# A gated two-part layer (state-space mixer, then a spiking feed-forward): the mixer's output computed feature-major in 512 columns, its second norm fetched through memory

## The chip, the cores and the metric

The kernel runs on one core of a Trainium2 chip. The core has five engines, each with its own queue of instructions, which it takes in order: TensorE (PE: matmuls, with its weight loads PEld), VectorE (DVE), ScalarE (ACT), GpSimd (POOL) and SyncE (SP), which here only issues DMAs. Operands lie in SBUF (128 partitions); matmuls write to PSUM, whose banks hold 128 x 512 fp32 values. The time is device microseconds (us) of one execution, lower is better. It is given as the median of several runs, and one further execution is profiled.

## The reference

For 16 sequences of 1024 tokens with 256 features, in fp32 (cut; the modulation `sa ... gb` is computed per sequence from a small input `c`, and `ga`, `gb` are clipped to at least 0.25 in size):

```python
h = _layernorm(x) * (1 + ca) + sa
Bu = (einsum('bti,ni->btn', h, W_B) + b_B) * dt          # 256 x 256
xs: x_t = A_bar * x_(t-1) + Bu_t                          # scan along the tokens
y = einsum('btn,on->bto', xs, W_C) + b_C + einsum('bti,oi->bto', h, W_D) + b_D
x = x + ga * y                                            # x1 below
h = _layernorm(x) * (1 + cb) + sb
y = square(relu(h @ W_fc.T)) @ W_proj.T                   # 256 -> 1024 -> 256
spikes: 5 steps of a leaky integrator driven by y, mean number of spikes per element
x = x + gb * spikes
```

## The kernel before

**Tiles.** The 16,384 tokens are cut into 32 tiles of 512 tokens (`TT`); two tiles make one sequence, and the scan carries its last column from the first to the second. Weights stay in SBUF, each as two fp32r halves (a rounded high part and the rest), and so do the moving operands: a product is three matmuls (`PASSES`: high x high, low weight x high, high weight x low) for each of the two 128-row blocks of the contraction (`products`, line 243).

**Layouts.** "Token-major" has tokens on the partitions, which the norm needs (its mean is along the free axis, `bn_stats`). "Feature-major" has features on the partitions, which matmuls, scan and the spike stage need. Two ways lead from one to the other. `transpose` (line 388) uses TensorE against an identity; it serves tiles 0 and 1 only. `hop` (line 342), through `turned` (line 346), has VectorE transpose 32 x 32 blocks, writes the result to device memory in four DMAs of 128 KB, and reads it back in one of 512 KB.

**The stages of a tile t**, by the names of the tiles in the profile:
- first norm of `xq` (a second copy of x in memory, laid out for `hop`): `moments`, `aggregate`, `root_in`, `root`, `root_inverse`, `newton`, `normalise` (xn_a, ScalarE), `hop` (w_a, hop_a, v_a), then `turned_hi` and `turned_lo` (lines 379, 382) give h_a, scaled, in two halves
- `state_input` (pb, 12 matmuls of 512 columns), `state_bias` (bu, ScalarE), `state_scan` (xs, VectorE), `state_hi` and `state_lo` (xsp)
- `mix_h` and `mix_xs` (lines 449, 455; py): here h_a and xsp stand as weights, in blocks of 128 tokens, and W_D and W_C move in 256 columns; y is token-major, in two PSUM tiles of 256 tokens (g = 0, 1). Each of the two makes 2 x 12 = 24 matmuls
- `residual` (line 398): GpSimd adds the bias row ga*(b_C + b_D + ...) to the loaded x, in place. `mix_out` (line 458): VectorE multiplies y by the row ga and adds that x: x1, token-major. The rows come broadcast over the partitions by `load_rows` (line 233) from a small table that the kernel writes at its start
- second norm of x1, by the same functions, and `hop` (w_b, hop_b, v_b), giving h_b
- `expand` (pf, 4 pairs of 2 x 6 matmuls; relu, square and the high half on ScalarE) with `hidden_lo` (hid, VectorE), and `contract` (pp, 4 pairs of 12 matmuls)
- `spike` (o, five VectorE operations for each half of the features), `gated` (ScalarE), and `output` (line 526; GpSimd adds x1, SyncE stores). `output` needs x1 feature-major, which `hop_residual` (line 359: w_x, hop_x, v_x) fetches by the same way as `hop`

**Order.** Nothing is left to a scheduler: all engines' handles are wrapped so that what is issued stays in program order (`InOrder`; so nearly all instructions in the profile have its line, 82). After set-up and a hand-written `first_period` (line 719), `period(t)` (line 839) is called for t = 1 to 30. It interleaves the stages of five tiles: spike, gate and output of t-1, expand and contract of t, second norm of t+2 with its hop in the next period, mix_xs and mix_out of t+2, state and mix_h of t+3, first norm of t+4. `last_tile` finishes. On TensorE a period reads: expand 0, expand 1, mix_xs, expand 2, contract 0, contract 1, expand 3, state_input, contract 2, mix_h, contract 3.

**Buffers.** PSUM: four banks `ps_f` (pf, pb), two `ps_y` (py), two `ps_p` (pp). `contract(t, 0)` therefore waits until both spikes of t-1 have read their pp. SyncE's queue is in order too: a DMA that waits for its data holds up those behind it.

Of the kernel before, what the change touches and what calls it, by code (L numbers as in the profile page):

```python
# [21 lines left out]
F32 = mybir.dt.float32  # L23
# [64 lines left out]
def adaln_kernel(ctx: ExitStack, tc: tile.TileContext, x, xq, w_bT, w_cT, w_dT, b_CD, w_fcT, w_projT,  # L88
                 cols, wmod, out):
# [19 lines left out]
    xts, xqs, bcs = {}, {}, {}  # L109

    def load(t):
        if t >= TILES:
            return
        xts[t] = io.tile([P, SUB, D], F32, tag="x", name=f"x_{t}", bufs=3)
        Q.dma_start(out=xts[t], in_=x[t])
# [9 lines left out]
    col = const.tile([P, KD * NB + 2 * KD + 1], F32, name="col")  # L125
    Q.dma_start(out=col, in_=cols)
    cs = col[:, 0:KD * NB].rearrange("p (k b) -> p k b", k=KD)
    la = col[:, KD * NB:KD * NB + KD]
    bb = col[:, KD * NB + KD:KD * NB + 2 * KD]
    ldt = col[:, KD * NB + 2 * KD:]  # L130
# [3 lines left out]
    load(0)  # L134
# [6 lines left out]
    spare = work.tile([NB, 8, D], F32, tag="hid", name="spare", bufs=HIDB)  # L141
    bcd, rows = spare[0:2, 0], spare[:, 2:5]
    Q.dma_start(out=fcm, in_=w_cT.rearrange("(k p) n -> p k n", p=P))
    Q.dma_start(out=bcd, in_=b_CD.rearrange("(n d) -> n d", n=2))
    load(1)
# [4 lines left out]
    load(2)  # L150
# [5 lines left out]
    first = spare[:, 5, 0:P]  # L156
    G.memset(first, 0.0)
    G.memset(first[0:1], 1.0)
    ones = spare[0:2, 7, 0:NB]
    G.memset(ones, 1.0)  # L160
# [11 lines left out]
    sb = const.tile([P, KD, NB], F32, name="sb")  # L172
    gb = const.tile([P, KD, NB], F32, name="gb")
# [5 lines left out]
    rows_a = dram.tile([NB, 2 * D], F32, name="rows_a")  # L179
# [40 lines left out]
    def gate(wm, name):  # L220
        ps = ps_f.tile([NB, D], F32, tag="ps_f", name=f"ps_{name}")
        for k in range(KD):
            PE.matmul(ps, lhsT=sil[:, k], rhs=wm[:, k, 2 * D:], start=k == 0, stop=k == KD - 1)
        return ps

# [6 lines left out]

    def load_rows(b):
        bc = io.tile([P, 2, D], F32, tag="bc", name=f"bc_{b}", bufs=2)
        Q.dma_start(
            out=bc.rearrange("p n d -> p (n d)"),
            in_=rows_a[b:b + 1, :].rearrange("o e -> (o e)").partition_broadcast(P),
        )
        bcs[b] = bc
# [18 lines left out]

    def moments(key, src, between=lambda: None, blocks=range(SUB)):
        if key not in norms:  # L260
            n = norms[key] = Norm()
            n.sts = [small.tile([P, 6], F32, tag=f"st{s}{key[0]}", name=f"st_{key}_{s}", bufs=2)
                     for s in range(SUB)]
        for s in blocks:
            V.bn_stats(norms[key].sts[s], src[:, s])
            between()
# [56 lines left out]
    def normalise(key, src):  # L323

        n = norms.pop(key)
        xn = work.tile([P, SUB, D], F32, tag="xn", name=f"xn_{key}", bufs=3)
        for s in range(SUB):
            S.activation(xn[:, s], src[:, s], AF.Identity, bias=n.m[:, s:s + 1], scale=n.r[:, s:s + 1])
        xns[key] = xn

    def normalise_by(key, src, engines):
# [3 lines left out]
        for s, E in enumerate(engines):  # L335
            if E is S:
                S.activation(xn[:, s], src[:, s], AF.Identity, bias=n.m[:, s:s + 1], scale=n.r[:, s:s + 1])
            else:
                E.tensor_scalar(xn[:, s], src[:, s], n.r[:, s:s + 1], n.m[:, s:s + 1], ALU.mult, ALU.add)
        xns[key] = xn  # L340

    def hop(key):

        vs[key] = turned(key, xns.pop(key), "turned", 3)

    def turned(key, src, tag, bufs):


        w = work.tile([P, D // 32, SUB, 32], F32, tag="xn", name=f"w_{key}", bufs=3)
        V.transpose(w.rearrange("p j s u -> p s j u"), src.rearrange("p s (j r) -> p s j r", r=32))  # L350
# [4 lines left out]
        v = work.tile([P, KD, TT], F32, tag=tag, name=f"v_{key}", bufs=bufs)  # L355
        Q.dma_start(out=v, in_=d.rearrange("(k p) t -> p k t", p=P))
        return v

    def hop_residual(t):
        xfs[t] = turned(f"x{t}", x1s.pop(t), "xf", 2)  # L360
# [27 lines left out]
    def transpose(key, pool=ps_f, tag="ps_f"):  # L388

        xn = xns.pop(key)  # L390
        for k in range(KD):
            ps = pts[key, k] = pool.tile([P, TT], F32, tag=tag, name=f"pt_{key}_{k}")
            for s in range(SUB):
                PE.transpose(ps[:, s * P:(s + 1) * P], xn[:, s, k * P:(k + 1) * P], ident)

    ys, vs, xns, hs, xbs, xss, xsps, x1s, xfs, relus, hids, accs, outs = ({} for _ in range(13))

    def residual(t, half, E=G):

        b = t // 2  # L400
        xt = xbs[t] = xts[t]
        xt = xt[:, 2 * half:2 * half + 2]
        E.tensor_tensor(xt, xt, bcs[b][:, 1:2].to_broadcast([P, 2, D]), ALU.add)
# [35 lines left out]
    def mix_part(t, g, w, a, first, last):  # L439


        for late in range(2):
            for j in range(2):
                cols = slice((2 * g + j) * P, (2 * g + j + 1) * P)
                products(ys[t, g][:, j], lambda i, k: w[:, i, k], lambda i, k: a[:, i, k, cols],
                         first and j == 0 and not late, last and late == 1, False,
                         PASSES[2:] if late else PASSES[:2], True)

    def mix_h(t, g):
        if g == 0:  # L450
            x1s[t] = work.tile([P, SUB, D], F32, tag="x1", name=f"x1_{t}", bufs=3)
        ys[t, g] = ps_y.tile([P, 2, D], F32, tag="ps_y", name=f"py_{t}_{g}")
        mix_part(t, g, wd, hs[f"a{t}"], True, False)

    def mix_xs(t, g):
        mix_part(t, g, wc, xsps[t], False, True)

    def mix_out(t, g):

        b = t // 2  # L460
        dst = x1s[t][:, 2 * g:2 * g + 2]
        V.tensor_tensor(dst, ys.pop((t, g)), bcs[b][:, 0:1].to_broadcast([P, 2, D]), ALU.mult)
        V.tensor_tensor(dst, dst, xbs[t][:, 2 * g:2 * g + 2], ALU.add)


    def expand_begin(t, pair):
# [9 lines left out]
        def rest(part):  # L476
            if part == 0:
                for j in range(2):
                    src, dst = ps[j], a[:, j]
                    if t == 0:  # L480
                        src = src.rearrange("p (s q u) -> p q s u", q=P // 32, s=SUB)
                        dst = dst.rearrange("p (q s u) -> p q s u", q=P // 32, s=SUB)
                    S.activation(dst, src, AF.Relu, bias=bias_f[:, 2 * pair + j, b:b + 1])
# [42 lines left out]
    def output(t, at, E=G):  # L526
# [4 lines left out]
        if E is G:  # L531
            G.tensor_tensor(o, o, xfs[t][:, m, cols], ALU.add)
        else:
            V.scalar_tensor_tensor(o, o, gb[:, m, b:b + 1], xfs[t][:, m, cols], ALU.mult, ALU.add)
        Q.dma_start(out=out[t, :, m, cols], in_=o)

    def last_tile(t):
# [4 lines left out]
        hop_residual(t)  # L542
# [72 lines left out]
    moments("a0", xts[0], between=lambda: decay(1))  # L615
# [15 lines left out]
    normalise_by("a0", xts[0], (V, S, V, S))  # L631
# [8 lines left out]
    ps_ga = gate(wm1, "ga")  # L640
    scaled_lo("a0", lambda k: pts["a0", k])
    V.tensor_tensor(wd[:, 1], fd, wd[:, 0].bitcast(F32), ALU.subtract)
    clipped(ps_ga, rows[:, 0], spare[:, 6], 1.0)
    S.activation(wc[:, 0], fcm, AF.Copy)
    state_input(0)

    ps_bd = ps_p.tile([NB, D], F32, tag="ps_p", name="ps_bd")
    PE.matmul(ps_bd, lhsT=ones, rhs=bcd, start=True, stop=False)
    for k in range(KD):
        PE.matmul(ps_bd, lhsT=sa[:, k], rhs=fd[:, k], start=False, stop=k == KD - 1)  # L650
    state_bias(0)
    state_scan(0, (0,))
    V.tensor_tensor(rows[:, 1], ps_bd, rows[:, 0], ALU.mult)
    Q.dma_start(out=rows_a, in_=rows[:, 0:2].rearrange("b n d -> b (n d)"))
    load_rows(1)
    mix_h(0, 0)

    ps_bc = ps_p.tile([P, 2, D], F32, tag="ps_p", name="ps_bc")
    PE.matmul(ps_bc.rearrange("p n d -> p (n d)"), lhsT=first, rhs=rows[:, 0:2].rearrange("b n d -> b (n d)"),
              start=True, stop=True)  # L660
    mix_h(0, 1)
# [5 lines left out]
    bcs[0] = io.tile([P, 2, D], F32, tag="bc", name="bc_0", bufs=2)  # L667
    S.activation(bcs[0], ps_bc, AF.Copy)
    state_lo(0, slice(1, 2))
    for half in range(2):  # L670
        residual(0, half, V)
    mix_xs(0, 0)
    mix_out(0, 0)
    moments("b0", x1s[0], blocks=(0, 1))
    mix_xs(0, 1)
    mix_out(0, 1)
    ps_cb = columns(wm2, 1, "cb")
    ps_sb = columns(wm2, 0, "sb")
    S.activation(sb, ps_sb, AF.Copy)
    moments("b0", x1s[0], blocks=(2, 3))  # L680
# [4 lines left out]
    moments("a1", xts[1], blocks=(0, 1))  # L685
    newton_v("b0")
    V.tensor_scalar(s2, ps_cb, 1.0, None, ALU.add)
    normalise_by("b0", x1s[0], (V, S, V, S))
# [3 lines left out]
    ps_bf = ps_p.tile([P, KF, NB], F32, tag="ps_p", name="ps_bf")  # L692
# [12 lines left out]
    moments("a1", xts[1], blocks=(2, 3))  # L705
# [11 lines left out]
    load(3)  # L717

    def first_period():
# [4 lines left out]
        normalise_by("a1", xts[1], (V, S, V, S))  # L724
# [3 lines left out]
        moments("a2", xqs[2])  # L728
        aggregate("a2")
        hop_residual(0)  # L730
# [7 lines left out]
        for half in range(2):  # L738
            residual(1, half)
# [9 lines left out]
        normalise("a2", xqs[2])  # L749
        hop("a2")  # L750
        load_q(4)
        for half in range(2):
            residual(2, half)
        for g in range(2):
            mix_h(1, g)
# [6 lines left out]
        moments("a3", xqs[3])  # L762
# [4 lines left out]
        halves(wp, fp, *proj(1))  # L767
        halves_lo(wp, fp, *proj(1), V)
        halves(wf, ff, *fc(3))
        halves_lo(wf, ff, *fc(3), V)  # L770
        r2(2)
        for g in range(2):
            mix_xs(1, g)
# [3 lines left out]
        for g in range(2):  # L777
            mix_out(1, g)
        contract(0, 1)
        normalise("a3", xqs[3])  # L780
        hop("a3")
        load_q(5)
        moments("b1", x1s[1])
        aggregate("b1")
        root_in_v("b1")
        root("b1")
        newton_v("b1")
# [177 lines left out]
```

## Time and profile before

| | |
|---|---|
| median of 3 runs | 1027.45 us (1024.75 to 1027.96) |
| profiled execution, its own time | 1027.32 us |
| its span, first to last instruction | 1025.5 us |
| mean granted TensorE clock | 0.991 |
| ScalarE busy | 771.9 us (75%) |
| GpSimd busy | 387.9 us (38%) |
| mean DMA traffic | 152 GB/s |

Lines that start with two times are from a timeline: start in us from the span's start, us taken, engine, line, operation, written tile <- read tiles, shapes, count; in brackets the idle time before it and what ended it. Neighbouring equal instructions are merged, so the time is that of the group up to the end of its last one; the distance between two starts is the better measure of the pace. "SPq" is SyncE issuing DMAs; the time shown is that of issuing, not of the transfer. The chain of waits is followed back from the last instruction, at each step to what released it.

A few more figures of the page, used below:

```profile
L82 ACT ACTIVATE a<-pf,bias_f 128x512 f32<-128x512 f32 (+1 forms) x264 | 169.2, 668 | 110.6 <-PE pf L82 109.4
L82 POOL TENSOR_TENSOR x<-x,bc 128x512 f32<-128x512 f32 x62 | 79.6, 1304 | 4.4 <-ACT xn_a L82 4.4
```

```profile
x<-in_x SPq DMA_DIRECT2D x32, 512.0 KB, 4.9
xq<-in_xq SPq DMA_DIRECT2D x30, 512.0 KB, 5.7
v_b<-hop_b SPq DMA_DIRECT2D x31, 512.0 KB, 3.6
```

In the first two the columns are: what, count | busy us in all, mean ns of one | idle time of the engine before it and what ended most of it. In the last three: count, KB each, median us from issue to landing.

### The profile page before, as it was taken

Reading aid. Unit: us, or ns where it says so; the run is one execution under the profiler, and the core shown is the slowest. Engines: PE = TensorE matmul, PEld = TensorE weight load, DVE = VectorE, ACT = ScalarE, POOL = GpSimd, SP = SyncE. Lnnn points to the kernel's source line nnn. Section 1 sums busy time; section 2 is a strip of 40 time slices with the busy share of each in tenths; the row PEclk is TensorE's granted clock in tenths of the full one; section 3 lists DMA queues with packets and bytes.
Section 4 is the critical chain, followed back from the end, with each engine's and each line's share of the span. In section 5 each row is a group of like instructions: output and inputs, shape, how many; then the busy total and the mean of one; then the engine's idle time right before and its main releaser. Section 6 shows DMA issues by size and latency. Waiting matters only on the chain.

```text
span 1025.5 us, 15207 instructions
## 1 busy us (share of the span) xinstructions
PE 1006.9 (98%) x5208; PEld 860.4 (84%) x5208; DVE 934.6 (91%) x1573; ACT 771.9 (75%) x1154; POOL 387.9 (38%) x529
## 2 busy tenths in 40 slices
PE   9999899999999999999999999999999999999996
PEld 6977788888888888888888888888888888888886
DVE  6888999999999999999999999999999999998775
ACT  4556787877787787787777778778778877776775
POOL 0300444344553343554334455434355433444211
PEclk9899999999999999999999999999999999999998
DMA  7234456546545645455655554564555555543332
GB/s 250 81 103 154 124 175 185 158 140 179 158 146 175 182 148 153 146 167 160 186 152 158 160 157 155 164 192 137 164 150 157 166 175 166 148 139 94 103 104 83
DMA packets 150531, 156.27 MB, mean 152 GB/s; under 512 B 10018, under 2 KB 108324, under 8 KB 150452
## 3 DMA queue, kind: packets, MB, share of 16 engines
q1 hardware_dynamic: 150452, 155.28, 50.3%
q8 instruction: 41, 0.67, 0.3%
q14 instruction: 38, 0.31, 0.1%
HBM read 89.67 MB, written 65.57 MB: 151 GB/s over the span
## 4 chain that ended last, share of the span: by engine, by line
PE 90%; DVE 5%; DMA 2%; ACT 1%; issue 1%; SPq 0%; POOL 0%; DVEq 0%; ACTq 0%; POOLq 0%
PE pf L82 32%; PE pp L82 32%; PE py L82 16%; PE pb L82 8%; DVE o L82 1%; DVE xs L82 1%; PE ps_bf L82 1%; DVE hid L82 1%; DMA wm<-in_wmod 1%; ACT a L82 1%; SPq L82 0%; DMA v_a<-hop_a 0%; DMA v_b<-hop_b 0%; DVE w_a L82 0%; DVE h_a L82 0%
## 5 line engine op out<-in xcount | busy, mean ns | idle before, releaser
L82 PE MATMUL pp<-hid,wp 128*128 128x512 f32 (+1 forms) x1584 | 369.3, 385 | 6.1 <-DVE o L82 2.3
L82 PE MATMUL pf<-h_b,wf 128*128 128x512 f32 (+1 forms) x1584 | 367.0, 384 | 0.0
L82 PEld LDWEIGHTS pp<-hid,wp 128*128 128x128 f32 x1584 | 289.4, 189 | 66.4 <-DVE o L82 2.7
L82 PEld LDWEIGHTS pf<-h_b,wf 128*128 128x128 f32 x1584 | 289.9, 189 | 57.2 <-DVE h_b L82 0.5
L82 POOL TENSOR_TENSOR o<-o,v_x 128x512 f32<-128x512 f32 x64 | 109.4, 1731 | 452.3 <-ACT o L82 428.4
L82 ACT ACTIVATE a<-pf,bias_f 128x512 f32<-128x512 f32 (+1 forms) x264 | 169.2, 668 | 110.6 <-PE pf L82 109.4
L82 DVE TENSOR_TENSOR hid<-a,hid 128x1024 fp32r<-128x1024 f32 (+1 forms) x132 | 194.1, 1472 | 13.1 <-ACT hid L82 13.1
L82 DVE SCALAR_TENSOR_TENSOR o<-pp,o 128x512 f32<-128x512 f32 (+1 forms) x260 | 177.6, 683 | 8.9
L82 ACT ACTIVATE hid<-a 128x1024 fp32r<-128x1024 f32 (+1 forms) x132 | 136.7, 1036 | 4.2
L82 ACT ACTIVATE a<-a 128x1024 f32<-128x1024 f32 (+1 forms) x132 | 136.7, 1036 | 4.2
L82 PEld LDWEIGHTS py<-wc,xsp 128*128 128x128 f32 x768 | 96.2, 191 | 6.8 <-ACT xsp L82 3.9
L82 PE MATMUL py<-wc,xsp 128*128 128x256 f32 x768 | 98.2, 283 | 2.7 <-ACT xsp L82 2.6
L82 PEld LDWEIGHTS py<-wd,h_a 128*128 128x128 f32 x768 | 96.3, 191 | 3.6 <-issue 1.2
L82 PE MATMUL py<-wd,h_a 128*128 128x256 f32 x768 | 97.5, 283 | 0.0
L82 PE MATMUL pb<-h_a,wb 128*128 128x512 f32 x384 | 93.6, 392 | 0.0
L82 PEld LDWEIGHTS pb<-h_a,wb 128*128 128x128 f32 x384 | 72.7, 190 | 16.3 <-issue 0.8
L82 POOL TENSOR_TENSOR x<-x,bc 128x512 f32<-128x512 f32 x62 | 79.6, 1304 | 4.4 <-ACT xn_a L82 4.4
L82 DVE TENSOR_SCALAR o<-pp 128x512 f32<-128x512 f32 (+1 forms) x65 | 43.2, 664 | 38.5 <-PE pp L82 33.4
L82 ACT ACTIVATE xn_b<-x,m_b,r_b 128x256 f32<-128x256 f32 x126 | 65.6, 591 | 7.5 <-POOL m_b L82 2.7
L82 ACT ACTIVATE xn_a<-xq,m_a,r_a 128x256 f32<-128x256 f32 x120 | 62.1, 593 | 2.5 <-POOL m_a L82 1.5
L82 ACT ACTIVATE xsp<-xs 128x1024 fp32r<-128x1024 f32 (+1 forms) x33 | 34.1, 1034 | 36.2 <-DVE xs L82 36.2
L82 DVE TENSOR_TENSOR x<-x,x 128x512 f32<-128x512 f32 x64 | 53.2, 832 | 6.5
(131 smaller groups left out, 962.0 us busy)
## 6 DMA issues: line engine op xcount, KB each, us to landing
x<-in_x SPq DMA_DIRECT2D x32, 512.0 KB, 4.9
hop_x<-w_x SPq DMA_DIRECT2D x128, 128.0 KB, 2.5
v_x<-hop_x SPq DMA_DIRECT2D x32, 512.0 KB, 4.0
out<-o SPq DMA_DIRECT2D x63, 256.0 KB, 2.5
hop_b<-w_b SPq DMA_DIRECT2D x124, 128.0 KB, 2.9
v_b<-hop_b SPq DMA_DIRECT2D x31, 512.0 KB, 3.6
xq<-in_xq SPq DMA_DIRECT2D x30, 512.0 KB, 5.7
hop_a<-w_a SPq DMA_DIRECT2D x120, 128.0 KB, 3.7
```

The source lines that it names most:

```text
L82: return self.tc.keep_in_program_order(issue(*args, **kwargs))
```

## The change

- W_D and W_C stand as weights; h_a and xsp move, 512 columns at a time. `mix_h` and `mix_xs` make 12 matmuls each, into two PSUM tiles py (one per 128 features), so y is feature-major.
- `mix_out` becomes two ScalarE activations, x1 = ga * y + gac, with ga and gac = ga*(b_C + b_D + ...) as per-partition columns, and two adds of x (GpSimd; VectorE for tiles 0 and 1). x is now loaded feature-major, in two buffers instead of three. `residual`, `load_rows`, `gate`, the table of rows and the broadcast DMAs go.
- x1 stays feature-major, in four buffers, and `output` adds it as it is; `hop_residual` goes. The second norm needs x1 token-major: `hop_back` (VectorE transpose, four writes of 128 KB, one read of 512 KB into xm, one buffer) fetches it. Its statistics are taken at the start of the next period, and `normalise` and `hop` of the same tile follow in that period, after mix_out.
- Tiles 0 and 1 use TensorE: `transpose_back` for x1, `transpose` for their h_b. Tiles 0 and 1 also take the first norm from xq, and the permutation of tile 0's tokens is made by TensorE's transposes instead of the relu.
- In `first_period` weights' halves, norms and loads are put in another order; the second norm of tile 2 leaves it.
- On SyncE a period reads: out, hop_b (4), v_b, out, x, xq, hop_x (4), xm, hop_a (4), v_a. Before it was: hop_b (4), v_b, out, out, x, xq, hop_x (4), v_x, hop_a (4), v_a, and in every second period the rows.

```diff
-    def hop_residual(t):
-        xfs[t] = turned(f"x{t}", x1s.pop(t), "xf", 2)
+    def hop_back(t):
+        w = work.tile([P, P // 32, SUB, KD, 32], F32, tag="xn", name=f"w_x{t}", bufs=3)
+        V.transpose(w.rearrange("p q s m r -> p m (q s) r"),
+                    x1s[t].rearrange("p m (j u) -> p m j u", u=32))
+        d = dram.tile([P, SUB * D], F32, tag="hop_x", name=f"hop_x{t}", bufs=2)
+        dv = d.rearrange("(q u) (f c) -> f u q c", u=32, f=P // 32)
+        for f in range(P // 32):
+            Q.dma_start(out=dv[f], in_=w[32 * f:32 * f + 32].rearrange("u q s m r -> u q (s m r)"))
+        v = work.tile([P, P // 32, SUB, KD * 32], F32, tag="xm", name=f"xm_{t}", bufs=1)
+        Q.dma_start(out=v.rearrange("p f s c -> p (f s c)"), in_=d)
+        xms[t] = lambda s: v[:, :, s]
...
-    def mix_part(t, g, w, a, first, last):
-        for late in range(2):
-            for j in range(2):
-                cols = slice((2 * g + j) * P, (2 * g + j + 1) * P)
-                products(ys[t, g][:, j], lambda i, k: w[:, i, k], lambda i, k: a[:, i, k, cols],
-                         first and j == 0 and not late, last and late == 1, False,
-                         PASSES[2:] if late else PASSES[:2], True)
+    def mix_part(t, w, v, first, last):
+        for passes in (PASSES[:2], PASSES[2:]):
+            for m in range(KD):
+                products(ys[t, m], lambda i, k: w[:, i, k, m * P:(m + 1) * P], lambda j, k: v[:, j, k],
+                         first and passes[0] == PASSES[0], last and passes[0] != PASSES[0], True, passes, True)
...
-    def mix_out(t, g):
+    def mix_out(t, E=G):
         b = t // 2
-        dst = x1s[t][:, 2 * g:2 * g + 2]
-        V.tensor_tensor(dst, ys.pop((t, g)), bcs[b][:, 0:1].to_broadcast([P, 2, D]), ALU.mult)
-        V.tensor_tensor(dst, dst, xbs[t][:, 2 * g:2 * g + 2], ALU.add)
+        x1 = x1s[t] = work.tile([P, KD, TT], F32, tag="x1", name=f"x1_{t}", bufs=4)
+        for m in range(KD):
+            S.activation(x1[:, m], ys.pop((t, m)), AF.Identity, bias=gac[:, m, b:b + 1], scale=ga[:, m, b:b + 1])
+        for m in range(KD):
+            E.tensor_tensor(x1[:, m], x1[:, m], xts[t][:, m], ALU.add)
...
     def period(t):
-        if t % 2 == 0 and four:
-            load_rows((t + 4) // 2)
         spike(t - 1, accs.pop((t - 1, 0)), (0, 0))
         if one:
-            hop(f"b{t + 1}")
+            moments(b1, xms[t + 1])
+            aggregate(b1)
+            root_in(b1, G)
         expand(t, 0)
+        if one:
+            root(b1)
         spike(t - 1, accs.pop((t - 1, 1)), (1, 0))
         expand(t, 1)
+        if one:
+            root_inverse(b1)
+            newton(b1, G)
+        hidden_lo(t, 0)
         gated(t - 1, (0, 0))
-        output(t - 1, (0, 0))
-        hidden_lo(t, 0)
         if four:
-            moments(a4, xqs[t + 4])
+            moments(a4, blocks_of(xqs[t + 4]))
         hidden_lo(t, 1)
+        if two:
+            mix_xs(t + 2)
+            mix_out(t + 2)
+        output(t - 1, (0, 0))
+        if one:
+            normalise(b1, xms[t + 1])
+            hop(b1)
         gated(t - 1, (1, 0))
         output(t - 1, (1, 0))
+        load(t + 3)
+        load_q(t + 5)
         if three:
             turned_hi(a3)
-        if two:
-            mix_xs(t + 2, 0)
-            mix_out(t + 2, 0)
-            mix_xs(t + 2, 1)
-            mix_out(t + 2, 1)
-        load(t + 4)
-        load_q(t + 5)
         expand(t, 2)
         if four:
             aggregate(a4)
             root_in(a4, G)
         if three:
-            for half in range(2):
-                residual(t + 3, half)
             turned_lo(a3)
         contract(t, 0)
-        if two:
-            moments(b2, x1s[t + 2])
         if four:
             root(a4)
-        if one:
-            turned_hi(f"b{t + 1}")
-        if four:
             root_inverse(a4)
-        if two:
-            aggregate(b2)
-            root_in(b2, G)
-        if four:
             newton(a4, G)
         hidden_lo(t, 2)
         contract(t, 1)
-        if one:
-            turned_lo(f"b{t + 1}")
-        hop_residual(t)
+        if two:
+            hop_back(t + 2)
         expand(t, 3)
-        if two:
-            root(b2)
         hidden_lo(t, 3)
-        if two:
-            root_inverse(b2)
-            newton(b2, G)
         if three:
             state_input(t + 3)
             state_bias(t + 3)
             state_scan(t + 3)
+        if one:
+            turned_hi(b1)
+            turned_lo(b1)
         if four:
-            normalise(a4, xqs[t + 4])
+            normalise(a4, blocks_of(xqs[t + 4]))
             hop(a4)
         contract(t, 2)
         if three:
             state_hi(t + 3)
             state_lo(t + 3)
-            for g in range(2):
-                mix_h(t + 3, g)
-        if two:
-            normalise(b2, x1s[t + 2])
+            mix_h(t + 3)
         contract(t, 3)
```

## The prediction

> **What bounds the kernel now.** I read the page's busy table, then the chain of waits, then TensorE's timeline in a middle period (one 512-token tile), then the in-order queues that feed it.
>
> ```profile
> PE 1006.9 (98%) x5208; PEld 860.4 (84%) x5208; DVE 934.6 (91%) x1573; ACT 771.9 (75%) x1154; POOL 387.9 (38%) x529
> ```
>
> TensorE (PE) is busy nearly throughout, VectorE (DVE) is close behind. The chain of waits in the middle holds nothing but TensorE, and its timeline has no gap:
>
> ```profile
> 481.04 2.88 PE L82 MATMUL pb<-h_a,wb 128*128 128x512 f32 x12
> 483.76 2.88 PE L82 MATMUL pp<-hid,wp 128*128 128x512 f32 x12
> 486.48 3.04 PE L82 MATMUL py<-wd,h_a 128*128 128x256 f32 x24
> 489.35 2.91 PE L82 MATMUL pp<-hid,wp 128*128 128x512 f32 x12
> ```
>
> From start to start, 12 matmuls of 512 columns take 2.72 us (226.7 ns each) and 24 of 256 take 2.87 (119.6 each). The py groups start every 30.28 us (183.84 and 214.12 in the chain of waits): that is the period. VectorE has about 1.2 us of it to spare, waiting for the last pp:
>
> ```profile
> 461.63 0.69 DVE L82 TENSOR_SCALAR o<-pp 128x512 f32<-128x512 f32 x1 [1.17 <-PE pp L82]
> 462.35 2.87 DVE L82 SCALAR_TENSOR_TENSOR o<-pp,o 128x512 f32<-128x512 f32 x4
> 465.14 1.23 DVE L82 STREAM_TRANSPOSE w_b<-xn_b 128x1024 f32<-128x1024 f32 x1
> ...
> 473.95 0.68 DVE L82 TENSOR_TENSOR x<-py,bc 128x512 f32<-128x512 f32 x1
> 474.73 1.00 DVE L82 TENSOR_TENSOR x<-x,x 128x512 f32<-128x512 f32 x1
> ...
> 480.30 2.07 DVE L82 TENSOR_TENSOR hid<-a,hid 128x1024 fp32r<-128x1024 f32 x1
> ```
>
> One spike takes 3.5 us (461.63 to 465.14). The hid at 480.30 takes 2.07 instead of 1.2 because a GpSimd (POOL) add runs: two-input operations of the two engines take turns. SyncE's queue:
>
> ```profile
> 484.88 1.84 SPq L82 DMA_DIRECT2D hop_x<-w_x  x4
> 488.90 0.38 SPq L82 DMA_DIRECT2D v_x<-hop_x  x1
> 489.43 2.01 SPq L82 DMA_DIRECT2D hop_a<-w_a  x4
> 494.49 0.38 SPq L82 DMA_DIRECT2D v_a<-hop_a  x1
> ```
>
> With nothing in front, four hop writes need 4.02 us until the read back can be issued (484.88 to 488.90). With v_x in front they need 5.06: transfers queue.
>
> **The change, part by part.** *Matmuls.* mix_h and mix_xs lose 24 x 256 columns each and get 12 x 512: 2 x (2.87 - 2.72) = 0.30 us; the group after each starts at 2.72 rather than 2.75, so the floor is 132 x 0.2267 = 29.92, 0.36 less than 30.28. Over 28 periods this is 10 us, the only saving on the engine that bounds. Against it stands the Trainium skill (TensorE: Matmul & The Clock Gate, Back-to-back issue gap), whose isolated gap is N/2.4 + 2.5 ns. By that rule the two groups would save only 0.06 us a period and the whole some 2 us. The trace's pitches have a fixed part of 12.5 ns (119.6 less the 107.1 by which the two pitches differ), so I take the 0.36.
>
> *VectorE* loses mix_out, 2 x (0.68 + 0.69 to 1.00) = 2.7 to 3.4 us a period. It gains nothing: the 32x32 transpose of hop_residual (1.23) becomes hop_back's. *ScalarE (ACT)* gains two x1 activates, nearest row a<-pf at 0.62 each from start to start: 1.25 us, on 79% busy; it fits. *GpSimd* swaps two residual adds (1.27 each) for two x1 adds of the same shape. The strided statistics and normalise: same elements, priced as now (0.33 and 0.5 each), bounds -0.1 and +0.5 us; I take 0. The broadcast rows (15 DMAs of 256 KB), the gate rows and the first tile's permuted relu go; none is on the middle's chain.
>
> *The new dependency.* Now x1 goes to moments directly, and hop_residual's DMAs are needed only by the next period's output. After, hop_back's five DMAs stand between x1 and moments(b), and mix_out's GpSimd adds stand in front of output. In SyncE's new order hop_b waits behind the first out, and hop_x behind hop_b, v_b, the second out, x and xq. All engines are in order, so this closes a ring around the period. Its length, from the start of the b statistics (the mark):
> - four statistics and their aggregates, 1.30 + 0.29: 1.6
> - second spike 3.5: 5.1
> - reciprocal, then GpSimd's five small Newton operations, which wait behind hidden_lo (1.1) and then take 1.2: 7.5
> - two x1 adds with hidden_lo(t,1) taking its turn between them, like today's pair of o (3.54 from 471.64): 11.1; the first output add 1.27: 12.4
> - out issued, 0.4: 12.8; hop_b to v_b's issue, 4.22 (466.40 to 470.62): 17.0.
>
> From here two branches lead to the next mark.
>
> Branch A: v_b until ScalarE starts h_b, 4.0 to 4.2 (87.73 to 91.68; 61.41 to 65.62); h_b 1.23, the four xn_a behind it on ScalarE 2.07, VectorE's w_a 1.2 and xsp 1.15, the next first spike 3.5. Sum 17.0 + 4.1 + 9.15 = 30.25.
>
> ```profile
> 87.73 3.92 DMA v_b<-hop_b
> ...
> 96.86 1.30 DVE st_b L82 x4
> 98.15 0.29 DVE mv_b L82 x4
> ```
>
> Branch B: hop_x starts to issue 1.8 us after v_b, with v_b, out, x and xq (1.79 MB, 3.5 times 512 KB) in flight ahead. No row shows that stack. From below, 512 KB in front costs 1.63 us (303.19 to 307.13 alone, 307.13 to 312.70 with v_x): 3.94 + 3.5 x 1.63 = 9.65 until xm can be issued. From above, xq lands 6.2 us after x's issue (354.48; 5.7 after 354.95); less 2.0, the shortest landing of any transfer, this is 2.1 for 512 KB: 11.2. I take 1.63 for v_b and out and 1.9 for x and xq, since the latter's row has half an out in front: 10.2. Then xm's own landing 3.6 (v_b's median). Sum 17.0 + 10.2 + 3.6 = 30.8, ends 30.25 and 31.8.
>
> ```profile
> 303.19 1.84 SPq L82 DMA_DIRECT2D hop_x<-w_x  x4
> 307.13 0.38 SPq L82 DMA_DIRECT2D v_x<-hop_x  x1
> 307.74 1.96 SPq L82 DMA_DIRECT2D hop_a<-w_a  x4
> 312.70 0.38 SPq L82 DMA_DIRECT2D v_a<-hop_a  x1
> ```
>
> So the ring (30.8) is longer than TensorE's new floor (29.92) and than today's period (30.28). What is late then: xm, so moments and the second spike, whose PSUM contract(t,0) needs; TensorE stalls in front of pp some 0.9 us a period. Its cover, 2.5 us between spike and contract, is used up in three periods.
>
> *The start.* Today the second spike of tile 0 releases contract(1,0) at 109.26:
>
> ```profile
> 109.26 4.15 PE L82 MATMUL pp<-hid,wp 128*128 128x512 f32 x16 [2.29 <-DVE o L82]
> ```
>
> After, b1 goes through 16 TensorE transposes (1.04 for 8: 2.1 us, in gaps that exist) instead of over memory (83.70 to 91.66), w_p's halves move ahead of a wait of 1.5 us, and b2's statistics and normalise leave period 0 (3 us of VectorE). The first spike then starts near 94 instead of 101.0. But xm_2 lands only near 99: hop_a4 from 86, hop_x behind v_a from 91, xm issued at 95, 3.6 more. Mark at 99, contract(1,0) at 99 + 5.1 = 104.1: 5.2 earlier, bounds 0 and 8. The longer first-tile chain (x1 through ScalarE, 8 transposes, statistics only then) hides behind ps_bf's 28 small matmuls until 35.68; without that cover it costs 2 us.
>
> *Sum.* Today contract(28,0) starts at 927.1 (957.36 for tile 29, less 30.28). After: 99 + 26 x 30.8 + 30.25 (no xq load there, so branch A) + 5.1 = 935.2: 8.1 later. Tail: two groups in period 28 and one in 29 save 0.5, and h_b of tile 30, at the mark + 22, comes about 1 late. Net +8.6 on the profiled 1027.32 (span 1025.5; it is 0.1 below the median 1027.45): **1036 us**.
>
> **Rivals.** (1) Branch B is at its low end, so A's 30.25 decides: 99 + 27 x 30.25 + 5.1 = 920.9, 6.2 earlier, 1022; without the gain at the start 1027. For it: A's pieces are all rows. (2) The other side: the ring closes within 29.92, so TensorE keeps the clock and nothing stalls. Place: SyncE's queue from the first out to xm; it decides if hop_x loses less than 1.2 us to the transfers ahead and A is 0.4 shorter. 104.1 + 27 x 29.92 = 911.9, 15.2 earlier: 1012. For it: DMA engines are busy 54% on average, VectorE gets 3 us of room. Against: the trace's queueing. (3) B at its high end: 26 x 1.0 more, 1062. The matmuls do become 512 wide, so a change that does nothing is no rival.
>
> **How the numbers follow.** Forecast (B, 30.5 to 31.3: 1028 to 1049) 0.45; rival 1 0.23; rival 2 0.17; rival 3 0.15. A measurement tells 0.3% (3.1 us) from nothing. Faster: rival 2 and two thirds of rival 1, 0.31. Same: the rest of rival 1 and the forecast's lower edge, 0.12. Slower 0.57. Range 1013 to 1052: it leaves out the bottom of rival 2 and most of rival 3, about 0.2. The forecast's own range is 1028 to 1049.
>
> **What would show it.** py in two groups of 12 at 2.72; a pp wait on DVE o in every period, st_b waiting for the DMA xm; a period of 30.8; hop_x to xm near 8.5 us. Gapless TensorE at 29.92 would refute the ring; st_b never waiting while h_b waits for v_b would leave branch A.

## The result and the profile after

The changed kernel takes 1042.15 us in the median (1041.92 to 1043.48), the kernel before 1027.34 in the same runs: a ratio of 1.0152, 95% interval 1.0132 to 1.0171, so 1.3 to 1.7% slower. The profiled execution took 1042.31, its span is 1040.5, the mean granted clock 0.986. The medians below leave out two executions at a far lower granted clock than the rest (one with the Newton edit, 1667.24 at 0.559, and one of the kernel before, 1240.44 at 0.753).

Two lines of the page: busy time by engine, and the chain of work that ended last, by engine. Behind them the second line as it was for the kernel before:

```profile
PE 1007.0 (97%) x4468; PEld 819.9 (79%) x4468; DVE 884.7 (85%) x1439; ACT 807.5 (78%) x1217; POOL 341.9 (33%) x533
...
DVE 26%; PE 26%; DMA 20%; ACT 16%; issue 4%; POOL 4%; SPq 3%; DVEq 0%; POOLq 0%; ACTq 0%
```

```profile
PE 90%; DVE 5%; DMA 2%; ACT 1%; issue 1%; SPq 0%; POOL 0%; DVEq 0%; ACTq 0%; POOLq 0%
```

TensorE is as busy as before (1006.9) with 740 matmuls fewer; in the version without waits below it is 993.8, so some 13 us of short waits count as busy here. VectorE is 50 us less busy. The chain is the news: before, TensorE held 90% of it; now it passes from engine to engine. This is what a ring looks like in that view: no engine owns it.

One turn of it, in a middle period. VectorE's timeline:

```profile
496.35 1.41 DVE L81 BATCH_NORM_STATS2 st_b<-xm 128x6 f32<-128x256 f32 x4 [0.77 <-DMA xm<-hop_x]
...
501.43 0.17 DVE L81 RECIPROCAL q_b<-q_b 128x4 f32<-128x4 f32 x1
...
528.08 1.41 DVE L81 BATCH_NORM_STATS2 st_b<-xm 128x6 f32<-128x256 f32 x4 [1.32 <-DMA xm<-hop_x]
```

GpSimd's, where the two pairs of adds stand in front of the first store:

```profile
503.85 3.53 POOL L81 TENSOR_TENSOR x<-x,x 128x512 f32<-128x512 f32 x2
507.34 2.99 POOL L81 TENSOR_TENSOR o<-o,x 128x512 f32<-128x512 f32 x2
```

SyncE's queue, whole from the first store to xm:

```profile
508.65 0.36 SPq L81 DMA_DIRECT2D out<-o  x1
509.05 2.08 SPq L81 DMA_DIRECT2D hop_b<-w_b  x4
513.30 0.38 SPq L81 DMA_DIRECT2D v_b<-hop_b  x1
513.73 0.47 SPq L81 DMA_DIRECT2D out<-o  x1
514.24 0.43 SPq L81 DMA_DIRECT2D x<-in_x  x1
514.77 0.42 SPq L81 DMA_DIRECT2D xq<-in_xq  x1
515.24 2.63 SPq L81 DMA_DIRECT2D hop_x<-w_x  x4
523.26 0.34 SPq L81 DMA_DIRECT2D xm<-hop_x  x1
```

Read them as one path: mark (start of st_b) at 496.35, second spike done at 501.43, the x1 adds done at 507.38, the first out add done and its store issued at 508.65, only then hop_b, though its data, w_b, was there by 507.4 (VectorE's transpose starts at 506.15 and takes 1.23); v_b at 513.30; hop_x starts at 515.24 and is done 8.0 later, when xm can be issued; the next mark, at 528.08, waits for xm. In TensorE's timeline this arrives as

```profile
533.30 4.20 PE L81 MATMUL pp<-hid,wp 128*128 128x512 f32 x16 [0.42 <-DVE o L81]
538.00 1.21 PE L81 MATMUL pp<-hid,wp 128*128 128x512 f32 x4 [0.50 <-DVE hid L81]
```

a wait for the spike and, since VectorE is behind, one for hid. The waits summed over the run (us in all, how often, the longest):

```profile
ACT h_b L81 <- DMA v_b<-hop_b: 54.2, 30, 3.7
...
DVE st_b L81 <- DMA xm<-hop_x: 16.1, 16, 3.1
...
PE pp L81 <- DVE hid L81: 9.2, 22, 0.5
...
PE pp L81 <- DVE o L81: 7.9, 5, 3.8
```

From mark to mark the 27 middle periods take 30.90 us on average (834.40 in all); TensorE's work in one is 29.92.

### The profile page after: what moved, and what is told of

The parts are those of the page before. It is cut to its first block, busy times and chain, and to the rows that moved or that the text cites. A ratio compares the mean times of both kernels' runs of the same rounds, so it can differ in the third digit from the quotient of the medians.

```text
span 1040.5 us, 13678 instructions
## 1 busy us (share of the span) xinstructions
PE 1007.0 (97%) x4468; PEld 819.9 (79%) x4468; DVE 884.7 (85%) x1439; ACT 807.5 (78%) x1217; POOL 341.9 (33%) x533
## 4 chain that ended last, share of the span: by engine, by line
DVE 26%; PE 26%; DMA 20%; ACT 16%; issue 4%; POOL 4%; SPq 3%; DVEq 0%; POOLq 0%; ACTq 0%
DVE o L81 13%; PE pp L81 10%; DMA xm<-hop_x 8%; DMA hop_x<-w_x 8%; PE pf L81 7%; ACT a L81 6%; DVE st_b L81 4%; DVE hid L81 4%; PE py L81 4%; PE pb L81 4%; SPq L81 3%; POOL e_b L81 3%; ACT xn_b L81 2%; ACT hid L81 2%; ACT h_a L81 2%
## 5 line engine op out<-in xcount | busy, mean ns | idle before, releaser
L81 DVE TENSOR_TENSOR hid<-a,hid 128x1024 fp32r<-128x1024 f32 (+1 forms) x132 | 183.5, 1394 | 39.5 <-ACT hid L81 39.4
L81 ACT ACTIVATE a<-a 128x1024 f32<-128x1024 f32 (+1 forms) x132 | 136.7, 1036 | 4.2
L81 POOL TENSOR_TENSOR x<-x,x 128x512 f32<-128x512 f32 x60 | 104.0, 1754 | 11.3 <-ACT x L81 11.3
L81 POOL TENSOR_TENSOR o<-o,x 128x512 f32<-128x512 f32 x64 | 93.7, 1483 | 32.3 <-ACT o L81 28.0
L81 DVE SCALAR_TENSOR_TENSOR h_a<-v_a,s,h_a 128x512 fp32r<-128x512 f32 x60 | 95.2, 1625 | 0.8 <-ACT h_a L81 0.7
L81 PE MATMUL py<-xsp,wc 128*128 128x512 f32 x384 | 92.6, 390 | 0.3 <-ACT xsp L81 0.3
L81 PE MATMUL py<-h_a,wd 128*128 128x512 f32 x384 | 92.2, 389 | 0.0
L81 PEld LDWEIGHTS py<-xsp,wc 128*128 128x128 f32 x384 | 71.9, 188 | 15.5 <-ACT xsp L81 0.7
L81 PEld LDWEIGHTS py<-h_a,wd 128*128 128x128 f32 x384 | 72.1, 188 | 15.0
L81 ACT ACTIVATE h_b<-v_b,s 128x512 fp32r<-128x512 f32 x60 | 40.1, 716 | 54.2 <-DMA v_b<-hop_b 54.2
L81 ACT ACTIVATE xn_b<-xm,m_b,r_b 128x256 f32<-128x256 f32 x120 | 62.4, 591 | 5.6 <-POOL m_b L81 3.4
```

The lines of the kernel that those rows point to most:

```text
L81: return self.tc.keep_in_program_order(issue(*args, **kwargs))
```

## The experiments

All times are medians; ratios are to the kernel before, run beside it on the same chip. "Mean period" is the mean of the 27 distances between marks from tile 2 to tile 29 in the trace.

### The order on SyncE's queue

Loads behind xm:

```diff
-        load(t + 3)
-        load_q(t + 5)
...
         if two:
             hop_back(t + 2)
+        load(t + 3)
+        load_q(t + 5)
```

> The loads of x and xq are issued behind xm instead of ahead of hop_x; nothing else moves. Ring theory: branch B (hop_x queued behind 1 MB of loads) loses some 4 us and never decides again; branch A (v_b, h_b, xn_a, w_a, xsp, spike) stays at 30.4 us from mark to mark, against 30.90 on the mean now. 27 marks x 0.5 = 13.5 us less: about 1029 us, st_b never waiting for xm, h_b still waiting for v_b in every period. Rival (shared SBUF port: VectorE and GpSimd taking turns set the period, the DMA wait is only a symptom): no change, 1042 us.

Measured: 1025.74, ratio 1.0003 (0.9986 to 1.0020), mean period 30.24. The same stretch of the queue:

```profile
507.54 0.47 SPq L81 DMA_DIRECT2D out<-o  x1
508.10 2.39 SPq L81 DMA_DIRECT2D hop_x<-w_x  x4
513.44 0.34 SPq L81 DMA_DIRECT2D xm<-hop_x  x1
513.82 0.43 SPq L81 DMA_DIRECT2D x<-in_x  x1
514.30 0.43 SPq L81 DMA_DIRECT2D xq<-in_xq  x1
```

From hop_x to xm it is 5.3 instead of 8.0, and st_b waits for xm in no middle period any more. The period falls to the length that the prediction gave branch A (30.25). Moving two loads past five DMAs, with not a byte less, takes back all that the change lost; the time is 3 us better than expected.

hop_b ahead of the first store:

```diff
-        output(t - 1, (0, 0))
         if one:
             normalise(b1, xms[t + 1])
             hop(b1)
+        output(t - 1, (0, 0))
```

> The first output (its GpSimd add stays behind the x1 adds) is issued on SyncE behind hop_b and v_b instead of ahead of them. Ring theory: hop_b starts when w_b is there, 11.1 us after the mark instead of 12.7. Branch A falls from 30.4 to 28.8, under TensorE's 29.92. Branch B gains 1.6 but gets the 256 KB of the first out ahead of hop_x, 0.8 back: about 30.1. So B alone decides, xm is waited for in nearly every period, h_b hardly waits: 27 x 0.75 = 20 us less, about 1022 us. Rival (shared port): no change, 1042.

Measured: 1016.75, ratio 0.9913 (0.9888 to 0.9938), mean period 29.91. What lies ahead of v_b gets shorter, and both branches lie behind v_b:

```profile
498.02 1.82 SPq L81 DMA_DIRECT2D hop_b<-w_b  x4
502.02 0.38 SPq L81 DMA_DIRECT2D v_b<-hop_b  x1
502.44 0.94 SPq L81 DMA_DIRECT2D out<-o  x2
```

hop_b starts 11.1 behind the mark instead of 12.7, and no store is in front of it, so v_b follows 3.9 later instead of 4.25. The expectation let branch B win 1.6 and lose 0.8 to the store that now stands ahead of hop_x. In the trace xm is issued 25.5 behind the mark instead of 26.8; with the landing of 3.8 this is 29.3, below TensorE's floor of 29.92. A wait for xm now and then (10 in all, 7.2 us) reaches TensorE in no middle period. The time is 5 us better than expected.

Both:

> Both edits. Ring theory: A is 28.8, B near 27, so TensorE decides with 29.92 per period: 27 x 0.98 = 26.5 us less, and the last two periods, whose chain from the mark to h_b is longer than their matmuls, lose some 2 us too: 1013 to 1016 us, TensorE without a gap in the middle, faster than the kernel before by some 1.2%. Rival (shared port): 1042. Rival (total DMA traffic, not its order): the bytes are the same, so no more than half of the gain.

Measured: 1015.82, ratio 0.9900 (0.9875 to 0.9925); every period from 186 to 934 is 29.92, TensorE without a gap. The same version once more:

> The version with both queue edits (hop_b ahead of the first out, loads behind xm) unaltered, for a time in this batch: 1014 to 1017, every middle period 29.92.

Measured: 1016.16, ratio 0.9901 (0.9881 to 0.9921), periods 29.92. That is 1% faster than the kernel before, where the change as made is 1.5% slower; the difference is the place of three calls.

### More load inside the ring, and outside it

One more 512 KB load a period, read by nothing, ahead of hop_x:

```diff
         load_q(t + 5)
+        junk = work.tile([P, KD, TT], F32, tag="junk", name=f"junk_{t}", bufs=1)
+        Q.dma_start(out=junk, in_=x[t])
```

> The changed kernel with one more load of 512 KB a period (read by nothing) issued behind x and xq, so ahead of hop_x. Theory (SyncE's queue from v_b to xm is a link of the ring): xm can be issued 1.6 to 2.1 later in 29 periods, the period goes from 30.9 to 32.3 to 33.0, since 0.5 of it was branch A's slack in some periods: 1080 to 1100. Rival (VectorE and GpSimd taking turns, or ScalarE, sets the period): no change, 1042 to 1045.

and the same two lines behind `hop_back(t + 2)`:

> The changed kernel with the same additional load of 512 KB a period, issued behind xm, ahead of hop_a. Theory: same traffic as in the run with the load ahead, but outside the ring, since v_a has most of a period to spare: 1042 to 1045. Rival (it is the sum of traffic that makes transfers late, wherever they stand): as late as with the load ahead, 1080 or more.

Measured: ahead 1072.98, ratio 1.0471 (1.0450 to 1.0492), mean period 31.92; behind 1039.24, ratio 1.0131 (1.0107 to 1.0155), mean period 30.80, no slower than the changed kernel. Same bytes, and only the place counts: this rules out the sum of traffic. And the period follows the queue with no operation of VectorE, GpSimd or ScalarE changed, so their taking turns, which is a part of the ring, is not by itself what sets it. The direction is as the theory has it, the size is not: the additional load was to make xm's issue 1.6 to 2.1 later and makes it 1.0 to 1.3 later.

```profile
528.36 0.38 SPq L81 DMA_DIRECT2D v_b<-hop_b  x1
...
530.28 0.72 SPq L81 DMA_DIRECT2D junk<-in_x  x1
531.05 1.99 SPq L81 DMA_DIRECT2D hop_x<-w_x  x4
538.86 0.34 SPq L81 DMA_DIRECT2D xm<-hop_x  x1
```

From v_b to xm's issue the medians are 6.27 with no load between (the first run above), 9.96 with x and xq (the changed kernel), 10.93 with three. Four more traces with the queue of the changed kernel up to xm (its second, and those of the runs with the load behind, the wait filled and the Newton edit alone) give 9.62 to 9.92, so a median is good to some 0.3. The first two loads cost 1.7 to 1.85 each on average (one alone was not run), the third 1.0 to 1.3. Why the third is cheaper was not settled.

### The 512 columns by themselves

The version with both queue edits, each group of mix cut again into 24 matmuls of 256 columns:

```diff
-                products(ys[t, m], ...
+                for c in range(2):
+                    cut = slice(c * TT // 2, (c + 1) * TT // 2)
+                    products(ys[t, m][:, cut], ...
```

> As the kernel with both edits, but every product of mix_h and mix_xs is cut into two matmuls of 256 columns, weights still standing: 48 matmuls of 256 in place of 24 of 512. If the fixed part of 12.5 ns per matmul is the saving, the period goes from 29.92 to 30.22 or 30.28, and the time up by 9 to 11 us on that kernel, to about 1024. By the rule of 2.5 ns fixed it goes up by about 2 us. If TensorE does not decide there, nothing changes.

Measured: 1026.75, ratio 1.0007 (0.9993 to 1.0021), 10.9 more than the version with 512 columns. Periods are 30.28:

```profile
513.49 3.04 PE L81 MATMUL py<-h_a,wd 128*128 128x256 f32 x24
516.36 2.91 PE L81 MATMUL pp<-hid,wp 128*128 128x512 f32 x12
519.11 5.60 PE L81 MATMUL pf<-h_b,wf 128*128 128x512 f32 x24
```

Start to start 2.87 and 2.75, as before the change; 0.36 a period, over 30 periods 10.8. The saving that the prediction took from the pitches is real, and without it the new layout gains nothing even in a ring that closes. By the isolated gap of the Trainium skill (TensorE: Matmul & The Clock Gate, Back-to-back issue gap) it would have been an estimated 0.06 a period, some 2 us; here the measurement decides.

### The tail

The prediction allowed the tail +0.5 and it cost 5.5 (worked out in the next section). Two theories of the cause were tried. First, the small Newton operations of the last two periods on VectorE, on the version with both edits and on the changed kernel:

```diff
-            newton(b1, G)
+            newton(b1, G if three else V)
```

> The version with both queue edits, and in periods 29 and 30 the second norm's five small Newton operations on VectorE instead of GpSimd. Theory (in the last two periods TensorE has less work than the chain from the b statistics to h_b is long, so each us of that chain is a us of the end): in the version with both edits the five take 966.73 to 969.95 in period 30, mostly waiting for VectorE's hid to let GpSimd through; on VectorE five such operations take about 0.9, so h_b of tile 30 comes about 2.2 earlier and the time is about 1013.5 against 1015.8. Rival (the tail is bounded by TensorE's own work or by the last spike): no change, 1015.8.

> The changed kernel with that tail edit alone. Theory: h_b of tile 30 is 2.5 to 3 earlier (the five took 992.64 to 996.03 after a wait for both hid), so about 1039.3; the periods in the middle stay as they are, 30.9 on average. Rival: no change, 1042.

Measured: 1013.38, ratio 0.9885 (0.9866 to 0.9904), and 1039.37, ratio 1.0140 (1.0122 to 1.0158). Both numbers are those expected, and neither shows it: the intervals overlap those without the edit. In the trace of the second, the way from the mark of tile 31 (in period 30) to the first matmuls of the last tile takes 20.9 instead of 21.7, 0.8 and not 2.5 to 3 (the h_b that period 30 makes, which these expectations call tile 30's, is tile 31's): xn_b now waits for ScalarE's own queue. In period 29, which has the edit too, nothing is won: from the mark of tile 30 to its h_b it is 23.0 instead of 21.5. The lower time comes from middle periods that the edit doesn't touch (mean 30.75). So two were measured again side by side, the version with both queue edits and the Newton edit, for a trace of its tail, and the changed kernel itself:

> Both queue edits and the small Newton operations on VectorE in the last two periods, for a trace of the tail: if the chain from the b statistics to h_b sets the tail, h_b of tile 30 is 2.2 earlier and the time 2 less than in the run with both edits of this batch. Rival, formed since: in that version TensorE waits only 0.6 for this h_b, so that no more than 0.6 of it reaches the end.

> The changed kernel unaltered, for a second trace and a time in this batch: 1040 to 1044, mean of the middle periods 30.7 to 31.0, a wait for h_b at the start of period 30 of 1 to 3.5 us with a lower granted clock behind it.

Measured: 1015.51, ratio 0.9894 (0.9873 to 0.9915), against 1016.16 without the edit: no difference shown, as the rival had it. TensorE no longer waits for h_b of tile 31 there, but 0.46 for the spike and 1.16 for hid, which the five operations now hold up on VectorE:

```profile
969.75 5.51 PE L81 MATMUL pp<-hid,wp 128*128 128x512 f32 x16 [1.16 <-DVE hid L81]
```

These 16 matmuls take 5.35 from start to start where 3.63 is usual: the granted clock is 0.50 from 970 to 973. In the traces, from the mark of tile 30 to the end of the span, it is 78.6 with the edit and 80.1 and 79.5 in the two runs without, but 80.95 with the edit on the changed kernel against 80.2 in both traces without. So whether the edit gains a part of a us stays open. And the unaltered changed kernel took 1039.40, ratio 1.0138 (1.0114 to 1.0163), with a mean period of 30.75: the spread of its middle is as large as what was looked for.

Second, the clock. In the changed kernel TensorE waits 1.44 for h_b at the start of period 30, and its windows show (us from and to; length; busy and count of PE, PEld, DVE, ACT, POOL; granted clock; DMA share; GB/s):

```profile
980.00:984.00 4.00, 2.44 (x10) 1.45 (x9) 1.44 (x3) 1.33 (x2) 0.00 (x0) 1.00 0.63 184
984.00:988.00 4.00, 4.00 (x12) 3.18 (x11) 3.86 (x7) 1.12 (x2) 0.00 (x0) 0.57 0.40 133
```

12 matmuls in 4 us, a clock of 0.57. Filling the wait:

```diff
         contract(t, 3)
+        if t == TILES - 3:
+            spare = ps_y.tile([P, TT], F32, tag="ps_y", name="ps_spare")
+            for _ in range(7):
+                PE.matmul(spare, lhsT=wf[:, 0, 0, 0:P], rhs=wf[:, 0, 0, 0:TT], start=True, stop=True)
```

> The changed kernel with seven spare matmuls of 512 columns (1.6 us) at the end of period 29, into a free PSUM tile that nothing reads, where TensorE otherwise waits 1.44 for h_b of tile 30. In the changed kernel's trace the granted clock is 0.57 from 984 to 988, right behind that wait, and expand 0 to 2 of period 30 take 10.28 for 36 matmuls instead of 8.16. Theory (the idle TensorE loses its clock, and that is 2.1 of what the tail lost): the clock stays at 1.00, the 36 take 8.2 to 8.6, the time is about 2 shorter than the changed kernel's in the same batch. Rival (the 36 are slow since h_b's low half is late): they take 10 again, no change.

Measured: 1042.13, ratio 1.0154 (1.0131 to 1.0177), against the 1039.40 of the changed kernel beside it. The clock stays up and the 36 matmuls take 8.5 from start to start instead of 10.3, and the time does not fall:

```profile
984.00:988.00 4.00, 4.00 (x19) 3.25 (x18) 3.86 (x8) 2.54 (x4) 0.00 (x0) 1.00 0.41 133
```

```profile
982.87 8.64 PE L81 MATMUL pf<-h_b,wf 128*128 128x512 f32 x36
991.34 1.07 PE L81 MATMUL pp<-hid,wp 128*128 128x512 f32 x4
...
1001.98 3.03 PE L81 MATMUL pp<-hid,wp 128*128 128x512 f32 x12 [1.45 <-ACT hid L81]
...
1009.25 7.94 PE L81 MATMUL pf<-h_b,wf 128*128 128x256 f32 x59 [0.23 <-ACT h_b L81]
```

The 1.8 us turn into waits further on; the last tile starts at 1009.25, in the changed kernel at 1009.17. The half clock was a symptom here and cost nothing: its stretch lay off the path that ends last. The second trace of the unaltered changed kernel agrees: there the clock stayed at 1.00, and from contract(28,0) to the end it takes 103.4 instead of 103.9. The path is the ring's own last turn, from the mark of tile 31 to its h_b: 20.3 us in the changed kernel (987.48 to 1007.78), 20.4 with the wait filled, 20.0 with both edits. And the end follows this h_b: from its start to the end of the span it is 32.7 to 32.8 in these three, and 33.1 in the version with the Newton edit on top, where the chain that ends last runs through the 16 slow matmuls shown above. By this comparison their half clock cost an estimated 0.3 to 0.4. Which link of the path would have to go was not settled.

## Why the prediction was right, and where not

Forecast 1036 in a range of 1013 to 1052, slower; measured 1042.15, slower, by the mechanism that it named. That it lies no more than 6 off is in part luck: the errors of the start (-1.8) and of the middle (+3.3) partly cancel.

| step | predicted | measured in the changed kernel |
|---|---|---|
| TensorE's floor of a period | 29.92 | 29.92 (reached in the version with both edits) |
| mark to second spike, Newton, x1 adds | 5.1, 7.5, 11.1 | 5.1, 7.55, 11.0 |
| mark to hop_b, to v_b, to h_b | 12.8, 17.0, 21.1 | 12.7, 16.95, 21.15 |
| v_b to xm's issue, loads ahead | 10.2 (9.65 to 11.2) | 9.96 median, 10.07 mean |
| xm's landing | 3.6 | 3.8 |
| branch A, branch B | 30.25, 30.8 | medians 30.42 (12 periods without a wait for xm), 30.76 (15 with one) |
| mean period | 30.8 | 30.90; 30.75 in a second trace |
| mark of tile 2; contract(1,0) | 99; 104.1 | 97.18; 102.40 |
| contract(28,0) | 935.2 | 936.6 |
| contract(28,0) to the end, over before | +0.5 | +5.5 |

- **The ring** is confirmed link by link, and by the runs that shorten it (queue order) and lengthen it (a load ahead) with TensorE's time following. h_b waited for v_b in all 30 periods and st_b for xm in 16, so both branches take part. Of the 27 middle periods, the 15 that end with a wait for xm have a median of 30.76 and a mean of 31.20, the 12 others 30.42 and 30.54; the mean of 30.90 is a mixture, and not branch B alone, by which the sum went. With the loads behind xm, where no middle period waits for xm, the mean is 30.24.
- **The signs.** One that it named did not show: a wait of pp for `o` in every period. TensorE waited for `o` 5 times and for hid 22 times (the lines above); VectorE, late by the spike, comes late to hid. From hop_x to xm it is 7.9 in the median, where it said near 8.5.
- **The price of the transfers ahead of hop_x** was right in sum (3.4 to 3.7 for x and xq, taken as 3.8), but a third load at 1.0 to 1.3 shows that they don't simply add up. Its upper bound was mis-added and rests on a wrong reading: 3.94 and 3.5 times 2.1 are 11.3, and the shortest landing in that trace is 1.7 (an out), not 2.0; the measured value lies below either way. The mean lies above the median because in two periods between 815 and 900 it took 8.6 to 9.8 from hop_x to xm's issue, where 7.6 to 7.9 is the median (marks up to 33.2 apart), in both traces of the changed kernel; why is open.
- **The start**: 1.7 better than taken, inside its bounds of 0 and 8.
- **The tail is the term that was mis-sized.** Of the 6.4 by which the span exceeds the predicted 1034.1, 1.4 come from start and middle together (-1.8 for the mark of tile 2, +3.3 for the periods, -0.1), 5.0 from the tail. The prediction let h_b of tile 30 come 1 late and gave nothing for period 30, +0.5 in all; measured are +5.5. But TensorE's work falls in the last periods, as state and mix drop out, and the ring doesn't. Before, ScalarE and TensorE in the tail read

```profile
985.14 1.32 ACT L82 ACTIVATE h_b<-v_b,s 128x512 fp32r<-128x512 f32 x2
```

```profile
971.54 8.32 PE L82 MATMUL pf<-h_b,wf 128*128 128x512 f32 x36
...
993.88 7.60 PE L82 MATMUL pf<-h_b,wf 128*128 128x256 f32 x60
```

so ScalarE began h_b of tile 31 8.7 before the last tile began; after, it is 1.4:

```profile
1007.78 1.34 ACT L81 ACTIVATE h_b<-v_b,s 128x512 fp32r<-128x512 f32 x2 [2.35 <-DMA v_b<-hop_b]
```

```profile
982.58 10.44 PE L81 MATMUL pf<-h_b,wf 128*128 128x512 f32 x36 [1.44 <-ACT h_b L81]
...
1009.17 7.94 PE L81 MATMUL pf<-h_b,wf 128*128 128x256 f32 x59 [0.23 <-ACT h_b L81]
```

This h_b is what the last tile waits for: period 30 takes 26.6 instead of 22.3, period 29 1.4 more than before. The prediction had the chain's length (mark + 21.1) and TensorE's remaining work in its views, and did not set one against the other for the periods with less work.
- **Rivals.** The first, branch A alone at 1022, is the run with the loads behind xm: 30.24 a period, 1025.74. The second, a ring within 29.92 at 1012, is the version with both edits, 1015.82, with the tail as the rest. Its conditions were put as two; the run with hop_b first shows that a shorter path to v_b, which both branches share, is enough.
- **Matmul width**: 0.36 a period, as taken from the pitches.

## What to carry to other kernels

When a producer's result goes through memory and back within the loop, write the ring out, mark to mark, with every in-order queue that it passes, and compare its length with the bounding engine's work in each stage, the drained last periods among them. On a shared queue, transfers that nobody waits for (prefetches, stores) go behind those in the ring: here moving three calls turned 1.5% slower into 1% faster. A low clock or a slow group beside a wait is no loss until a run shows that the end follows it: at 984 it cost nothing, at 970 in the version with the Newton edit a little.

## What the runs showed that was not expected

The granted clock fell behind a wait of 1.44 us (0.57 for 4 us, above; in windows of 1 us it is 1.00 until 984, then 0.53, 0.50, 0.50 and 0.77), and did not behind one of 1.36 in the second trace of the changed kernel (1.00 in all four windows from 976 to 992). The Trainium skill (TensorE: Matmul & The Clock Gate, What's actually happening) has the half clock only after an idle window of about 3.4 us; a wait less than half as long was enough here. The length of the wait alone doesn't decide it: 1.16 was enough in the version with the Newton edit (0.46 of waiting and 4 matmuls ahead of it), and in the run with the load ahead a wait of 2.16 was followed by 0.58, but this longer one by 1.00:

```profile
1025.93 5.12 PE L81 MATMUL pp<-hid,wp 128*128 128x512 f32 x20 [2.31 <-DVE o L81]
```

What decides was not tried.

Three loads ahead of a hop delay it by 4.7 us and two by 3.4 to 3.7: here the cost of a place further back in the queue was not proportional to the bytes ahead.
